# Sparse graph attention on one core: the units of each batch's first pair in another order, the average of v one place later, and a longer lead for the last projections

## The chip, the core and the metric

The kernel runs on one core of a Trainium2 chip. The metric is the device time of one launch in microseconds (us). A core has five engines that run side by side, each through its own list of instructions in a fixed order: PE (TensorE, matmuls), DVE (VectorE), ACT (ScalarE), POOL (GpSimd, which here issues the gathers) and SP (SyncE, which issues plain transfers). An instruction that needs another engine's result waits for it, and all that stands behind it on its own engine waits too.

## The reference

One layer of attention over a graph, a residual and a normalisation, for 16 batches of 1024 nodes with 512 features and 8 heads of 64:

```python
q = (x @ Wq + bq).reshape(b, n, H, HD)
k = (x @ Wk + bk).reshape(b, n, H, HD)
v = (x @ Wv + bv).reshape(b, n, H, HD)
scores = jnp.einsum('bqhd,bkhd->bhqk', q, k) / jnp.sqrt(jnp.float32(HD))
scores = scores + (1.0 - adj)[None, None, :, :] * -1000000000.0
attn = jax.nn.softmax(scores, axis=-1)
out = jnp.einsum('bhqk,bkhd->bqhd', attn, v).reshape(b, n, d)
return out @ Wo + bo              # then layernorm(x + this)
```

adj is a 0/1 matrix of 1024 x 1024, the same for all batches, with few ones in most rows. All arithmetic that reaches the output is in fp32.

## The kernel before

**Data.** The kernel ranks the nodes by their number of edges and works on queries in that order, in 8 tiles of 128. A query has few keys, so instead of the whole score matrix the kernel gathers, for each tile, its first, second, third key and so on: one *block* is 128 queries with one key each. A block is one indirect transfer by POOL of 128 rows of k and v (`gather`, L1242), a product with q and a sum over each head on DVE (`products` L1263, `scores` L1267), an exponential on ACT (L1278), a weighting of v by ACT (eight small activations, L1291) or by DVE (L1295), and an addition on DVE (L1307) or, for the few queries with many keys, a matmul on PE (L1316, L1317). There are 530 blocks in all, 32 or 34 for each batch; a query without any edge takes the mean of v, which the kernel keeps as one more row of the table of k and v.

**Projections ("fronts").** Before a batch's blocks can be gathered, its k, v and q must lie in DRAM. The function `pair(b, j)` computes them for two tiles of 128 rows (j = 0 to 3). k and v of two tiles come from seven products in place of eight (a scheme of sums and differences of half matrices): the units, in order, are x, p6, x again, p7, z, p4, z again. A unit is two matmuls of 128x128 by 128x512 in fp32, which stand as four rows in the profile. Between them stand q0 and q1 (the q products of the two tiles, four matmuls each) and xt (the two transposes of x that the next pair needs). x and z are each one PSUM bank that is filled in two halves: first a product, which must be read out (x by ACT's copy e, L960; z by DVE's L975, which makes v of the second tile), and then a second product added on top, read out again. So the second half of x waits for the copy e and the second half of z waits for L975. p6, p7, p4, all q and output products, the transposes, the average and others share four PSUM banks in turn (`fill_psum`).

In a batch's first pair (j = 0) from batch 1 on, q1 is empty. For even batches from 2 on q0 is empty too; for odd batches from 3 on q0 is the q product of a tile that two batches share, followed by `lone_product`, four bf16 matmuls.

After a batch's last pair `add_v` adds the last v tiles to vsum (L854), and `mean_pe` multiplies it by 1/N (matmul pm, L858); ACT copies the row and SP stores it (L864), and only then is the batch marked as set up, so that its blocks can be gathered.

**Outputs.** A finished tile is normalised (L1337), transposed (poT, L1351), multiplied by Wo (po, L790), added to x and normalised by DVE, ACT and POOL, and scattered to its rows. Twenty tiles are spilled to DRAM and finished after the fronts have ended.

**Order.** The whole order is written by one loop over *places* n, one for each block: at each place the loop emits the block work of nearby blocks, then what was put off to this place (`later(k, ...)` means k places on), and then PE work of fronts or outputs (`finish`) until a credit of PE time, `share`, is used up. `urgent` holds short PE work that goes ahead of it. A front unit has a condition (the second halves need e or v1 to have been emitted); if it is not met the place ends there. The share is set at each batch's first block, so that the fronts reach a given lead: `ahead` = 13 (EARLY) plus up to 11 (FIRST) places, less from batch to batch, beyond the batch after next. From batch 13's blocks on the share is what is left of the fronts, spread up to `fronts_end`, 12 places ahead of the last batch's first block. Gathers run 8 places ahead (AHEAD), 11 after the fronts' end (AHEAD_LAST), and not before the batch is set up. For odd batches from 3 on the first gather is `more` (L1217), which reads the table of both batches of a pair.

Of the kernel before, what the change touches and what calls it, by code (L numbers as in the profile page):

```python
# [46 lines left out]
LATE = 12  # L47
# [130 lines left out]
def kernel(  # L178
# [37 lines left out]
    B, N, D = x.shape  # L216
# [37 lines left out]
    with ExitStack() as main:  # L254
# [185 lines left out]
        now, plan, rest, urgent, known, waiting, combined = [0], {}, {}, [], [], [], []  # L440

        def later(k, fn):
            plan.setdefault(now[0] + k, []).append(fn)
# [363 lines left out]
        def pair(b, j):  # L807
# [25 lines left out]
            def send(i):  # L833
                assert b < PAIRED_FROM or gathered[0] >= start[max(0, b // 2 * 2 - 2)]
                kv = KV[b, tt[i]]
                rows, base = kv_of(b)
                for lo, hi in ((0, LONE), (LONE + P, 2 * P)) if b and tt[i] == 0 else ((tt[i] * P - (LONE if b and tt[i] == 1 else 0), None),):
                    hi = lo + P if hi is None else hi
                    part = slice(0 if lo % P == 0 or hi - lo == P else LONE, P if hi - lo == P or lo else LONE)
                    later(1, lambda lo=lo, hi=hi, part=part: nc.sync.dma_start(rows[base + lo:base + hi, :], kv[part, :]))  # L840
                R["sent"] = R.get("sent", 0) + 1
                if R["sent"] == 2:
                    later(1, add_v)
                    if j == NT // 2 - 1:
                        later(2, lambda: urgent.append(mean_pe))

            def add_v():
                kv = [KV.pop((b, t))[:, D:] for t in tt]
# [56 lines left out]
            if j == 0 and b >= PAIRED_FROM:  # L905
                q0 = []
# [29 lines left out]
            def a(i, h):  # L936
                return XT[b, tt[i]][:, ts(h, HD2)]

            def unit(bank, left, right, first, after, need):
                def pe():  # L940
                    if first:
                        R[bank] = fill_psum(f"p{bank}_{b}_{j}") if bank[0] == "p" else psum.tile(
                            [P, HALF], F32, tag=bank, name=f"{bank}_{b}_{j}", bufs=1
                        )
                    l = left()
                    for c in range(2):
                        nc.tensor.matmul(  # L947
                            R[bank], l[:, ts(c, P)], right[:, c, :], start=(first and c == 0), stop=(c == 1),
                            skip_group_check=True,
                        )  # L950
                    later(1, after)

                return [(2 * PRODUCT, pe, lambda: (need is None or need in R) and (b, j) in SX and bool(combined))]
# [28 lines left out]
            def s(i):  # L982
                return lambda: SX[b, j][i - 1]

            units = []
            units += unit("x", lambda: a(0, 0), B11, True, out_e, None)
            units += unit("p6", s(2), T2, True, out_w, None)
            units += q0
            units += unit("x", lambda: a(0, 1), B21, False, lambda: out_k(0, R["x"]), "e")
            units += unit("p7", s(3), T3, True, out_g, None)  # L990
# [472 lines left out]
        with tc.manual_schedule():  # L1463
# [9 lines left out]
            def needed(b, part):  # L1473
                b += int(part)
                if b >= B:
                    return fronts_time
                return fronts_by[b - 1] + (part - int(part)) * (fronts_by[b] - fronts_by[b - 1])

            finishing, last_finish, reloads, last_reload = [], -LEAD_IN, 0, 0
            fronts_end = start[B - 1] - 12  # L1480
            credit = 0.0
            for t in range(3):
                load_x(0, t)
# [1 line left out]
            while n < total or plan or rest or urgent or done or finishing or spilled or lone_tiles or not guarded:  # L1485
                now[0] = n
                if n < 0:
                    share = START_SHARE if n > FRONT_BY else LEAD_SHARE if n > -LEAD_IN else TRANSPOSE * 1.5
                elif n >= start[LATE + 1]:

                    share = sum(u[0] for u in fronts) / max(fronts_end - n, 1) + NS * SUM / NBT if fronts else LAST_SHARE
                elif n in start:

                    b = start.index(n)
                    left = sum(u[0] for u in fronts)
                    ahead = EARLY + FIRST * (1 - max(0, b - 1) / LATE)
                    goal = fronts_time - needed(b + 2, ahead / NBT)
                    kept = sum(number(b, t) not in SPILL for t in tiles_of(b))
                    share = (max(0.0, left - goal) + kept * NPAIR * PRODUCT + NS * SUM) / (start[b + 1] - start[b])
                if 0 <= n + 3 < total:  # L1500
                    exponentials(n + 3)
                if 0 <= n + 4 < total:
                    products(n + 4)
                while gathered[0] < min(n + (AHEAD if fronts else AHEAD_LAST) + 1, total) and blocks[gathered[0]][0] in set_up:
                    gather(gathered[0])
                    gathered[0] += 1
                if 0 <= n + 1 < total and not by_act(n + 1):
                    weigh(n + 1)
                if 0 <= n < total and blocks[n][2] < OWN[blocks[n][1]]:
                    add_own(n)  # L1510
                if 0 <= n + 4 < total:
                    scores(n + 4)
                if 1 <= n <= total and (n == total or blocks[n][2] == 0):
                    normalise(*blocks[n - 1][:2])
                if 0 <= n < total and blocks[n][1:] == one_key_at(blocks[n][0]):
                    turn(blocks[n][0], ONE_KEY, V1.pop(blocks[n][0]))
                if 0 <= n < total and blocks[n] == (B - 1, *MORE_AT):
                    turn(B - 1, MORE_TILE, V1.pop("more"))
                for fn in plan.pop(n, ()):
                    fn()  # L1520
                if 0 <= n + 2 < total and by_act(n + 2):
                    weigh(n + 2)
                for fn in rest.pop(n, ()):
                    fn()
                credit += paced(share, n) if n >= 0 else share
                if 0 <= n < total and blocks[n][2] >= OWN[blocks[n][1]]:
                    add_up(n)
                    credit -= SUM
                for tile_done in done[:0 if fronts and len(done) < LAZY else 1 if fronts else 2] + coming:
                    if tile_done not in loaded and kept_y() < 5:  # L1530
                        load_y(*tile_done)
                if lone_tiles and kept_y() < 4:
                    load_lone(lone_tiles.pop(0))
                coming[:] = [t for t in coming if t not in loaded]
                if spilled and not fronts and n > last_reload + 1 and len(Y) - kept_y() < 7:
                    reload(*spilled.pop(0), reloads)
                    reloads, last_reload = reloads + 1, n
                first_unit = True
                while credit > 0 or urgent:
                    if urgent and not (first_unit and fronts):  # L1540
                        urgent.pop(0)()
                        continue
                    if (
                        not finishing and len(done) > (LAZY if fronts else 0) and n > loaded.get(done[0], n) + 1
                        and n > last_finish + bool(fronts) and not total - 2 <= n < total
                    ):
                        finishing = finish(*done.pop(0))
                        last_finish = n
                    units = finishing or fronts
                    if not units:  # L1550
                        if urgent:
                            urgent.pop(0)()
                            continue
                        break
                    cost, fn, ready = units[0]
                    if ready and not ready():
                        if urgent:
                            urgent.pop(0)()
                            continue
                        break  # L1560
                    del units[0]
                    fn()
                    credit -= cost
                    first_unit = False
                credit = min(credit, 2 * share)
                while known and waiting:
                    load_x(*waiting.pop(0))
                preps += prep.pop(n, [])
                preps = [g for g in preps if next(g, True) is None]
                n += 1  # L1570
# [34 lines left out]
```

## Time and profile before

| | |
|---|---|
| median of 3 runs | 1875.09 us (1874.72 to 1876.87) |
| the profiled execution | 1894.52 us, of which the span from the first to the last instruction is 1892.4 |
| VectorE busy | 1695.3 us |
| ScalarE busy | 1557.4 us |
| POOL busy | 1262.6 us |
| q and output products (pq, po) on PE | 748.6 us |
| seven-product units (x, pp, z) on PE | 834.8 us in the page's groups |
| mean granted TensorE clock | 0.990 |

The profiled execution is some 19 us longer than the runs that give the time; sums are made against it. In lists of waits the columns are total us, times, longest. In a timeline each line is start and duration in us, engine, line of the kernel, operation, what it writes and reads, shapes, a count, and in brackets the idle time of the engine just before it and who ended it. In tables of stretches each engine has its busy us and instruction count; the last columns are the granted TensorE clock, the share of the DMA engines and GB/s. TensorE's ends are modelled, so small differences between busy shares carry little.

The page by slices shows the three stages: a setup until some 150 us, a long middle in which PE, DVE and ACT are all near full, and from some 1725 us a tail without fronts.

```profile
PE   7979999999999999999999999999999999999996
...
DVE  6888879999998999899999989899999989997875
ACT  3627868988888988988898878988899989977885
POOL 1366765777676776767676766767676866656884
PEclk9989999999999999999999999999999999999998
```

### The profile page before, as it was taken

What the parts mean: (1) busy time and instruction counts of PE and PEld (TensorE: products, weight loads), DVE (VectorE), ACT (ScalarE), POOL (GpSimd) and SP (SyncE); (2) the same over time, 40 slices, a digit from 0 to 9 for tenths busy, and PEclk for the clock granted to TensorE, in tenths of its full rate; (3) what the DMA queues carried; (4) which work ended last, traced back from release to release, by engine and by line L of the source; (5) the groups of instructions that cost most, each with busy time, mean ns of one, the idle gap of its engine ahead of it and who ended that gap; (6) DMA issues with size and microseconds to landing.
All of it is one profiled execution on the core that took longest, in us unless ns stands there. A gap on an engine that the chain in (4) does not pass through costs nothing. (4 is left out here: it accounts for less than half of the span.)

```text
span 1892.4 us, 25171 instructions
## 1 busy us (share of the span) xinstructions
PE 1816.5 (96%) x5149; PEld 876.6 (46%) x5149; DVE 1695.3 (90%) x3470; ACT 1557.4 (82%) x6128; POOL 1262.6 (67%) x1189
## 2 busy tenths in 40 slices
PE   7979999999999999999999999999999999999996
PEld 3434444444545454444444444444545444444442
DVE  6888879999998999899999989899999989997875
ACT  3627868988888988988898878988899989977885
POOL 1366765777676776767676766767676866656884
PEclk9989999999999999999999999999999999999998
DMA  7356786888989897989889897989889899989993
GB/s 279 115 167 215 226 290 229 309 298 291 322 266 319 303 333 256 345 290 310 299 284 329 279 324 261 334 303 309 286 302 352 297 332 319 329 282 319 340 332 137
DMA packets 188149, 544.63 MB, mean 288 GB/s; under 512 B 32602, under 2 KB 32622, under 8 KB 187986
## 3 DMA queue, kind: packets, MB, share of 16 engines
q0 software_dynamic: 116400, 382.82, 60.4%
q1 hardware_dynamic: 68510, 154.30, 21.7%
q10 hardware_dynamic: 3076, 5.82, 0.8%
q14 instruction: 120, 0.98, 0.2%
q8 instruction: 43, 0.70, 0.2%
HBM read 419.52 MB, written 144.34 MB: 298 GB/s over the span
## 5 line engine op out<-in xcount | busy, mean ns | idle before, releaser
L1291 ACT ACTIVATE pv<-kvg,pv 128x64 f32<-128x64 f32 x3544 | 893.4, 340 | 1.8 <-issue 1.8
L1242 POOL DMA_INDIRECT kvg<-kv_pair,place_row x462 | 522.6, 1131 | 258.6 <-issue 94.5
L790 PE MATMUL po<-wo,oT 128*128 128x512 f32 x816 | 379.2, 600 | 2.0 <-DVE vsum L854 1.2
L790 PE MATMUL pq<-wq,xT 128*128 128x512 f32 x792 | 369.4, 598 | 1.3 <-DVE s L1267 0.8
L1267 DVE TENSOR_REDUCE s<-qk 128x8 f32<-128x512 f32 x530 | 360.8, 681 | 7.2
L1263 DVE TENSOR_TENSOR qk<-qt,kvg 128x512 f32<-128x512 f32 x434 | 296.8, 684 | 13.2 <-DMA kvg<-kv_pair,place_row 13.1
L947 PE MATMUL x<-b,xT 128*128 128x512 f32 x504 | 239.0, 597 | 0.1
L947 PE MATMUL pp<-t,s 128*128 128x512 f32 x504 | 237.3, 593 | 1.5 <-DVE t L383 1.5
L1307 DVE TENSOR_TENSOR pv<-pv,pv 128x520 f32<-128x520 f32 x329 | 228.4, 694 | 8.2 <-ACT pv L1291 8.0
L790 PEld LDWEIGHTS po<-wo,oT 128*128 128x128 f32 x816 | 153.4, 192 | 171.7 <-issue 162.7
L790 PEld LDWEIGHTS pq<-wq,xT 128*128 128x128 f32 x792 | 149.0, 192 | 169.3 <-issue 157.7
L1001 POOL DMA_INDIRECT x<-in_x_dram,asked_row x120 | 129.6, 1080 | 103.5 <-PE pxT L748 35.4
L1278 ACT ACTIVATE pv<-s,absent 128x8 f32<-128x8 f32 x434 | 126.8, 293 | 55.1 <-DVE s L1267 36.6
L1125 POOL DMA_INDIRECT out_dram<-y,asked_row x129 | 145.1, 1125 | 35.9 <-issue 25.0
L800 ACT ACTIVATE sq_k<-kv 128x128 bf16<-128x128 f32 x512 | 150.8, 300 | 8.4 <-DVE kv L970 4.5
L947 PEld LDWEIGHTS x<-b,xT 128*128 128x128 f32 x504 | 95.3, 192 | 111.6 <-issue 105.2
L947 PEld LDWEIGHTS pp<-t,s 128*128 128x128 f32 x504 | 94.1, 190 | 111.3 <-issue 102.2
L947 PE MATMUL z<-b,s 128*128 128x512 f32 x252 | 121.4, 604 | 13.1 <-DVE kv L975 10.4
L1196 POOL DMA_INDIRECT qg<-q_rows,query_row x96 | 105.5, 1099 | 28.5 <-issue 25.3
L1029 POOL DMA_INDIRECT y<-in_x_dram,asked_row x93 | 105.0, 1129 | 26.1 <-issue 25.8
L947 PE MATMUL z<-t,s 128*128 128x512 f32 x252 | 118.6, 593 | 0.0
L947 PE MATMUL pp<-t,xT 128*128 128x512 f32 x252 | 118.5, 592 | 0.0
(276 smaller groups left out, 2750.2 us busy)
## 6 DMA issues: line engine op xcount, KB each, us to landing
kv_pair<-kv SPq DMA_DIRECT2D x98, 512.0 KB
q_rows<-q SPq DMA_DIRECT2D x106, 256.0 KB
qt<-q_rows SPq DMA_DIRECT2D x98, 256.0 KB
residual<-x SPq DMA_DIRECT2D x36, 256.0 KB
y<-residual SPq DMA_DIRECT2D x36, 256.0 KB
kv_rows<-kv SPq DMA_DIRECT2D x15, 512.0 KB
kvg<-kv_pair,place_row POOLq DMA_INDIRECT x462
kv_pair<-kv SPq DMA_DIRECT2D x28, 256.0 KB
```

Source lines behind the costliest of these rows:

```text
L790: nc.tensor.matmul(p, lhs(c), w[:, c, :], start=(c == 0), stop=(c == NPAIR - 1))
L800: nc.scalar.activation(sq, s[:, ts(h, P)], AF.Square, scale=scale, accum_out=sums[:, h:h + 1])
L947: nc.tensor.matmul(R[bank], l[:, ts(c, P)], right[:, c, :], start=(first and c == 0), stop=(c == 1), skip_group_check=True,)
L1001: nc.gpsimd.indirect_dma_start(out=y, out_offset=None, in_=x_rows, in_offset=bass.IndirectOffsetOnAxis(ap=asked_row[:, t:t + 1], axis=0), ...
L1125: nc.gpsimd.indirect_dma_start(out=out_rows[b, t], out_offset=bass.IndirectOffsetOnAxis(ap=rows, axis=0), in_=y, in_offset=None, element_o ...
L1196: nc.gpsimd.indirect_dma_start(out=q, out_offset=None, in_=q_rows[b % ROWS], in_offset=bass.IndirectOffsetOnAxis(ap=rows, axis=0))
L1242: nc.gpsimd.indirect_dma_start(out=KG[n], out_offset=None, in_=rows, in_offset=bass.IndirectOffsetOnAxis(ap=(place_row if b else key_row)[ ...
L1263: nc.vector.tensor_tensor(QK[n], q, KG[n][:, 0:D], op=OP.mult)
L1267: nc.vector.tensor_reduce(S[n], QK.pop(n).rearrange("p (h d) -> p h d", d=HD), axis=AX.X, op=OP.add)
L1278: nc.scalar.activation(PV[n][:, D:], S.pop(n), AF.Exp, bias=bias)
L1291: nc.scalar.activation(pv[:, ts(h, HD)], v[:, ds(D + h * HD, HD)], AF.Copy, scale=pv[:, D + h:D + h + 1])
L1307: nc.vector.tensor_tensor(PV[b, t], PV[b, t], pv, op=OP.add)
```

## The change

Three edits. In the first pair of each batch from 2 on, q0 is replaced by the first of the two x transposes, the place of xt is left empty, and the former q0 (with `lone_product`, where there is any) and the second transpose go between z's first half and p4. `mean_pe` is put off by three places instead of two for every batch but the first. And the fronts end 16 instead of 12 places ahead of the last batch, while `ahead` grows by 2 places at batch 11's first block and by 4 at batch 12's.

```diff
                 if R["sent"] == 2:
                     later(1, add_v)
                     if j == NT // 2 - 1:
-                        later(2, lambda: urgent.append(mean_pe))
+                        later(3 if b else 2, lambda: urgent.append(mean_pe))
...
             units = []
             units += unit("x", lambda: a(0, 0), B11, True, out_e, None)
             units += unit("p6", s(2), T2, True, out_w, None)
+            if j == 0 and b > 1:
+                q0, q1, xt = xt[:1], q0 + xt[1:], []
             units += q0
             units += unit("x", lambda: a(0, 1), B21, False, lambda: out_k(0, R["x"]), "e")
             units += unit("p7", s(3), T3, True, out_g, None)
             units += xt
             units += unit("z", s(1), T1, True, out_v1, None)
             units += q1
             units += unit("p4", lambda: a(1, 1), T4, True, out_k1, None)
             units += unit("z", s(4), B22, False, out_v0, "v1")
...
-            fronts_end = start[B - 1] - 12
+            fronts_end = start[B - 1] - 16
...
                     ahead = EARLY + FIRST * (1 - max(0, b - 1) / LATE)
+                    ahead += 2 * max(0, b - LATE + 2)
                     goal = fronts_time - needed(b + 2, ahead / NBT)
```

In the changed kernel lines from 985 on stand two lines lower, and the last ones three.

## The prediction

> **What bounds the kernel now.** I read the page's busy times first, then the busy time by stretches, then the waits of the tensor engine (PE), then the timelines at the batch boundaries. Page, then stretches:
>
> ```profile
> PE 1816.5 (96%) x5149; PEld 876.6 (46%) x5149; DVE 1695.3 (90%) x3470; ACT 1557.4 (82%) x6128; POOL 1262.6 (67%) x1189
> ...
> 300.00:1700.00 1400.00, 1372.04 (x3931) 666.46 (x3930) 1316.60 (x2578) 1240.91 (x5019) 971.05 (x897) 1.00 0.88 305
> ...
> 1535.00:1570.00 35.00, 30.11 (x85) 13.99 (x84) 31.04 (x59) 27.19 (x108) 22.73 (x22) 0.95 0.93 326
> ```
>
> From 300 to 1700 us PE is busy 98%, VectorE (DVE) 94%. PE's work is fixed, so time is won only by removing PE's idle stretches: 28 us of those 1400. DVE is nearly full too, so a stretch removed here can come back at the next thing DVE owes. The third line is the worst stretch: PE idles 4.9 of 35 us and part of it runs at half clock. Who ends PE's waits (us, times, longest):
>
> ```profile
> PE z L947 <- DVE kv L975: 10.4, 5, 3.9
> ...
> PE pm L858 <- DVE vsum L854: 2.7, 3, 1.2
> ...
> PE pxT L748 <- DVE q L821: 1.6, 2, 0.8
> ...
> PE po L790 <- DVE vsum L854: 1.2, 1, 1.2
> ...
> PE pm L858 <- ACT oT L1355: 1.1, 1, 1.1
> ```
>
> The largest is the second half of z, which adds to a bank that DVE must first read (L975). PE at batch 10's first pair:
>
> ```profile
> 1090.39 1.88 PE L947 MATMUL z<-t,s 128*128 128x512 f32 x4
> 1092.10 1.88 PE L947 MATMUL pp<-t,xT 128*128 128x512 f32 x4
> 1097.85 2.61 PE L947 MATMUL z<-b,s 128*128 128x512 f32 x4 [3.86 <-DVE kv L975]
> 1100.24 3.00 PE L947 MATMUL x<-b,xT 128*128 128x512 f32 x4
> ```
>
> Only one unit of 1.72 us stands between the halves. After the wait x takes 3.00 instead of 1.88: the clock was halved. And at batch 13's boundary POOL stops:
>
> ```profile
> 1520.93 0.87 POOL L1113 TENSOR_TENSOR stats<-stats,neg_half 128x1 f32<-128x1 f32 x1
> 1526.75 1.96 POOL L1217 DMA_INDIRECT more<-kv_pair,place_row  x1 [4.95 <-issue]
> ```
>
> SP issued the mean row's store at 1522.68; the gather from the same table starts 4.1 us later.
>
> **What the Trainium skill says.** "TensorE: Matmul & The Clock Gate", Part 1 (the HAM clock gate): the array falls to half rate after an idle window of about 3.4 us, and the window runs free. The trace shows the half rate (3.00 for 1.88), but it also follows idle stretches shorter than a window, 2.67 us before 877; so I price it from the trace: a half-clock stretch of 3.4 us loses 1.7. Same page, Architectural detail: VectorE and ScalarE are strict FIFO. Agrees: L975 stands behind a whole place's DVE work. "DMA: Bandwidth & Descriptors", Two DMAs through the same engine are not ordered: a dependent DMA has to wait for the first one's completion. That is the 4.95 us above.
>
> **The change part by part** (times of the profiled execution).
>
> *1. First pairs, batches 2 to 15.* No instruction is added. In even batches one x transpose (4 matmuls, 0.44 us) moves from ahead of the first half of z to between z's halves, the other to between p6 and the second half of x. In odd batches q0 (3.44) and lone_product (0.9) also move between z's halves. In the timelines of before, seven first pairs waited at z's second half: batches 4, 6, 7, 8, 10, 11, 12 with 0.54, 1.23, 1.34, 2.67, 3.86, 0.83, 1.45, in sum 11.9 us. In the changed program's order the PE work between the halves, at 0.86 per unit matmul, is 6.4 to 14.6 us in the odd batches (1.7 to 6.0 before), and 7.3 in batch 10, where sums and an output product fall in between: 7, 10 and 11 lose their 6.0. In 4, 6, 8 and 12 it grows only from 1.71 to 2.15: 4 x 0.43 = 1.7 gained, 4.2 left. Batch 14 shrinks from 3.4 to 2.15, and L975 now stands behind a whole place of DVE work; batch 12, with the same four operations ahead, had L975 end 3.3 after z's half, plus two y operations 1.3 = 4.6, so a new wait of 2.4 (0 to 3). Net -5.3 (range -9 to -2).
> Two half-clock stretches follow these waits, at 877 and 1099. The second goes, -1.7; the first stays, as batch 8 keeps 2.2 us.
> New tight places. (a) In odd batches q0 and lone_product no longer lie between x's halves, where ScalarE's copy e must come first. PE reaches the second half 4.3 us after x's start in batches 3, 7, 11, 13, 7.3 or later in 5, 9, 15. Before, e ended 4.5, 2.5, 3.6, 5.2 us after x's start in those four: waits 0.2 and 0.9, +1.1. (b) Four PSUM banks rotate; in batch 3 the transpose takes q0's bank 0.86 us after q0's last matmul, in batch 7 p4 takes it after 1.72. DVE's q (L821) must have read it a place later; the trace's two such waits (pxT <- q) are 0.8 each, with more PE work between. L975 lagged 1 to 6 us in first pairs; I take 2.0 and 1.0: +3.0 (0 to 8). x rows for the earlier transpose were gathered 40 us ahead in every batch, SP's order is nearly unchanged and DVE's four sums of halves (L774 to L777) now follow z: all nothing.
>
> *2. mean_pe a place later (b > 0).* vsum was late at 310, 1086, 1298, 1622 and 1731: 2.7 + 1.2 + 1.1 from the waits = -5.0 (-5 to -3). Its row is stored a place later; first gathers run 8 places ahead, and up to batch 12 the row still comes 12 or more places ahead, so four are left.
>
> *3. More lead for the last batches.* Counting places, the mean row of batches 13, 14, 15 comes 12, 12, 11 ahead of the batch's first block instead of 9, 8, 8. So the POOL stop of 4.95 (2.86 at batch 15) goes. Behind it stood two x gathers and the next key gathers; DVE then waited for keys at 1538.7 and 1543.3 (1.47, 1.53), and PE idled 0.66 at 1541.9, 1.63 at 1558.8, 2.46 at 1565.4, with 1.7 lost to half clock: 6.5 us. DVE's own backlog made part of these; I take two thirds, -4.3 (-6.5 to 0). Fronts end four places earlier; outputs move into the tail, where PE is the bound as well, so nothing; one output product takes the bias matmul, +0.2.
>
> Sum: -5.3 - 1.7 - 5.0 - 4.3 = -16.3; +1.1 + 3.0 + 0.2 = +4.3; net -12.0. DVE has 6% of its time free against PE's 2%, and in stretches (1570 to 1610: 39.3 of 40 us) nothing; there a gain comes back as a wait for DVE. I take 0.6 of the net: -7.2 us. The profiled execution took 1894.5 (span 1892.4), 19.4 above the median of the runs, 1875.1; I carry the difference over unchanged: 1867.9, say 1868.
>
> **The rivals.**
> - *DVE takes it back.* For: 94% busy, and most of PE's other waits end on DVE (poT <- o, sum <- pv). Against: DVE itself idles 83 us of the 1400, much of it waiting for PE. With 0.15 of the net, -1.8: 1873.
> - *Slower: x's second half waits for e.* Place: batches 3, 7, 11, 13, where the cover of 7 to 12 us is gone. If ScalarE is as late as the 7.1 us seen once (batch 5, third pair), each costs 2.8 plus a halved clock, 4.5: 18 us against 7.2: 1886. It decides from 1.8 us per place, e ending 6.1 after x's start. Against: among these four e ended at most 5.2 after.
> - *All of it.* The waits left in part 1 vanish as DVE is less behind, part 3 gives its 6.5 and nothing new appears: 11.9 + 3.4 + 5.0 + 4.8 (less the half clock counted) = 25; three quarters of that, -19: 1856.
> - *It does not do what it says:* in five even batches the halves stay only 2.15 apart; that is in the sum already.
>
> **How the numbers follow.** Main case 0.52 (1863 to 1872), taken back 0.22, e late 0.15, all of it 0.11. What the measurement can tell from no change is 0.2%, 3.75 us. Faster: the main case nearly whole (0.48), all of it (0.11), a little of the second (0.01): 0.60. Slower: e late, 0.15. Same: 0.25. For 8 in 10 the range reaches to "taken back" and a light form of "e late", and down to near "all of it": 1856 to 1878.
>
> **What would show it.** PE's waits for kv L975 fall from 10.4 to some 4 to 7, what is left lies in batches 4 to 14, even; pm's waits for vsum are gone; POOL's stop before L1217 (line 1219 after) is under 1 us; PE's busy share in 1535 to 1570 rises. Against it: ACT e named as what ends PE's waits for x, longer pxT <- q waits, more half-clock stretches between 200 and 1750 us than the four of before (at 266, 877, 1099, 1566), or the same idle sum under new names. I am wrong if PE's idle time between 200 and 1750 us does not fall by at least 5 us.

## The result: slower by 0.3%, and the profile after

The changed kernel takes 1881.92 us (median of 11 runs, 1877.68 to 1890.9) against 1875.57 of the kernel before beside it (11 runs): ratio 1.003, with an interval from 1.0019 to 1.0042. The prediction was 1868, with a range up to 1878; the time lies above both. A loss of 0.3% is small, but it is there, and it came back both times that the change was repeated: 1.0031 (1.0013 to 1.005) in e16 and 1.0042 (1.0028 to 1.0056) in e17.

The kernel before took 1875.6 to 1877.3 us in four of the six sessions of runs, 1897 and 1909 in the two others, and 1894.5 in the profile used for the prediction, so every ratio is to runs of the same session and traces are compared here with a repeat of the kernel before (e1, span 1875.6) and not with that profile.

This is the busy time of the changed kernel in two stretches (the stretch, its length, the busy time of PE, of its weight loads, of DVE, ACT and POOL, then granted clock, DMA share and GB/s):

```profile
300.00:1700.00 1400.00, 1380.48 (x3955) 672.26 (x3961) 1322.61 (x2583) 1241.64 (x5034) 976.46 (x899) 1.00 0.88 307
1535.00:1570.00 35.00, 35.00 (x103) 17.19 (x102) 34.55 (x68) 32.24 (x133) 21.44 (x21) 1.00 0.92 328
```

The same view of the repeat of the kernel before:

```profile
300.00:1700.00 1400.00, 1378.29 (x3956) 671.28 (x3955) 1323.32 (x2586) 1244.65 (x5041) 973.89 (x902) 1.00 0.88 307
1535.00:1570.00 35.00, 31.42 (x88) 14.62 (x87) 34.41 (x67) 29.35 (x116) 19.78 (x20) 0.95 0.88 300
```

Against the profile used for the prediction PE gains 8.4 us of busy time between 300 and 1700 us; against the repeat it gains 2.2. The stretch of batch 13 is as forecast (35.00 of 35 us), and already in the repeat it was less bad than the 30.11 I started from. These lines say who ends PE's waits in the changed kernel (us in total, times, longest):

```profile
PE pp L947 <- DVE s L776: 7.9, 4, 4.6
PE z L947 <- DVE kv L975: 6.6, 5, 2.6
...
PE poT L1353 <- DVE ends L1347: 5.8, 1, 5.8
PE sum L1318 <- DVE pv L1297: 4.7, 3, 2.2
PE po L790 <- DMA oTs<-spill: 3.0, 1, 3.0
...
PE pm L858 <- DVE vsum L854: 1.4, 1, 1.4
```

And in the repeat of the kernel before:

```profile
PE z L947 <- DVE kv L975: 8.5, 7, 3.9
...
PE pm L858 <- DVE vsum L854: 2.7, 3, 1.1
...
PE pm L858 <- ACT oT L1355: 1.1, 1, 1.1
```

Of the lines that are new, three are large: PE waits for a sum of halves (s, L776) 7.9 us, for the last attention block (poT, released by DVE's L1347) 5.8 us, and for the reload of a spilled tile 3.0 us. The first comes from edit 1, the others from edit 3, as the experiments below show. The longest wait of the first kind lies again in batch 10's first pair. Here is PE, and then DVE, of the changed kernel:

```profile
1078.22 0.60 PE L748 MATMUL pxT<-ident,x 128*128 128x128 f32 x4
1078.66 1.88 PE L947 MATMUL pp<-t,xT 128*128 128x512 f32 x4
1080.38 1.88 PE L947 MATMUL z<-b,s 128*128 128x512 f32 x4
1082.10 1.88 PE L947 MATMUL x<-b,xT 128*128 128x512 f32 x4
1083.81 0.60 PE L1353 MATMUL poT<-ident,o 128*128 128x128 f32 x4
1088.98 3.75 PE L947 MATMUL pp<-t,s 128*128 128x512 f32 x4 [4.57 <-DVE s L776]
```

```profile
1084.71 0.69 DVE L970 TENSOR_TENSOR kv<-pp,g 128x512 f32<-128x512 f32 x1
1085.31 0.68 DVE L1265 TENSOR_TENSOR qk<-qt,kvg 128x512 f32<-128x512 f32 x1
1085.91 0.69 DVE L1297 TENSOR_TENSOR pv<-kvg,pv 128x512 f32<-128x512 f32 x1
1086.51 0.72 DVE L1309 TENSOR_TENSOR pv<-pv,pv 128x520 f32<-128x520 f32 x1
1087.16 0.67 DVE L1269 TENSOR_REDUCE s<-qk 128x8 f32<-128x512 f32 x1
1087.76 0.41 DVE L774 TENSOR_TENSOR s<-xT 128x256 f32<-128x256 f32 x1
1088.09 0.41 DVE L775 TENSOR_TENSOR s<-xT,xT 128x256 f32<-128x256 f32 x1
1088.42 0.41 DVE L776 TENSOR_TENSOR s<-s,xT 128x256 f32<-128x256 f32 x1
```

z's second half (1080.38) no longer waits, as forecast. But the second transpose now runs at 1078.22. Its sums of halves (L774 to L777) stand on DVE behind a place of other work, which runs without an idle gap, and they start only at 1087.76. The second pair's p6 needs the third of them, L776, so PE stands idle for 4.57 us and then runs at half clock (3.75 us for a unit of 1.88). In the repeat of the kernel before, both transposes ran at 1068.84, and DVE did the same sums beside z's first half, well before z's second half at 1084.24:

```profile
1078.77 0.44 DVE L774 TENSOR_TENSOR s<-xT 128x256 f32<-128x256 f32 x1 [2.88 <-PE z L947]
...
1079.47 0.41 DVE L776 TENSOR_TENSOR s<-s,xT 128x256 f32<-128x256 f32 x1
```

This is the end of the changed kernel on PE:

```profile
1755.67 1.98 PE L790 MATMUL po<-wo,oTs 128*128 128x512 f32 x4 [2.96 <-DMA oTs<-spill]
...
1850.94 0.70 PE L1318 MATMUL sum<-pv,sums 128*128 128x256 f32 x2 [1.48 <-DVE pv L1297]
1851.48 0.61 PE L1319 MATMUL sum<-pv,sums 128*128 128x264 f32 x2
1857.88 1.09 PE L1353 MATMUL poT<-ident,o 128*128 128x128 f32 x4 [5.80 <-DVE ends L1347]
...
1860.12 5.10 PE L790 MATMUL po<-wo,oT 128*128 128x512 f32 x8 [0.85 <-ACT oT L1357]
```

And this is the end of the repeat of the kernel before:

```profile
1849.87 1.88 PE L790 MATMUL po<-wo,oTs 128*128 128x512 f32 x4
1851.58 0.59 PE L1316 MATMUL sum<-pv,sums 128*128 128x256 f32 x2
1852.02 0.61 PE L1317 MATMUL sum<-pv,sums 128*128 128x264 f32 x2
1854.88 0.66 PE L1351 MATMUL poT<-ident,o 128*128 128x128 f32 x4 [2.26 <-DVE o L1337]
...
1856.50 5.40 PE L790 MATMUL po<-wo,oT 128*128 128x512 f32 x8 [0.19 <-ACT oT L1355]
```

Before, products of reloaded tiles (oTs) lay between the last blocks' sums, up to 1851.58. After, they have run out at 1848.35, and PE waits for the last block's chain of work.

The wait at 1755.67 is for a reload that was issued late. In SyncE's list it stood behind the store of a mean output row (L1051), which waited 12.8 us for ACT's copy of that row; in the repeat the same store waited 6.6 us. SyncE in the changed kernel:

```profile
1736.58 0.43 SPq L1231 DMA_DIRECT2D qt<-q_rows  x1
1749.77 0.23 SPq L1051 DMA_DIRECT2D mean_rows<-out_mean  x1
...
1750.52 0.38 SPq L1057 DMA_DIRECT2D oTs<-spill  x1
```

The account can be kept with two points of the trace: the end of the last z, where the fronts end, and PE's last matmul. What lies between is the tail. Idle times in the table are PE's, all columns in us.

| profiled execution | last z ends | tail to PE's last matmul | PE's idle time from 200 us to last z | idle in the tail | span |
|---|---|---|---|---|---|
| before, repeated (e1) | 1707.8 | 154.1 | 21.7 | 8.8 | 1875.6 |
| changed kernel | 1701.1 | 164.1 | 21.1 | 15.8 | 1878.8 |
| edit 1 alone (e2) | 1711.6 | 154.9 | 26.4 | 9.8 | 1880.2 |
| edit 2 alone (e3) | 1708.0 | 154.5 | 20.6 | 9.0 | 1876.2 |
| edit 3 alone (e4) | 1702.1 | 166.5 | 20.2 | 14.0 | 1882.2 |
| edit 1, second transpose stays (e5) | 1702.5 | 154.2 | 19.0 | 9.3 | 1870.4 |

The changed kernel is 6.7 us earlier at the last z and takes 10.0 longer from there: +3.3, against a difference of the spans of 3.2.

Counting attention blocks by the start of their product with q on DVE shows where the time goes. After the last z 44 of the 530 blocks are still to come in the changed kernel, and 40 in the repeat, at 3.7 and 3.9 us of tail for each: the fronts end four blocks earlier, but only 6.7 us earlier. The last block starts 5.3 us later than in the repeat, and block 508 was already 6.1 us late. The 5.80 us that PE waits at the end are therefore not where the blocks fall behind; PE has then already done the products that it still had between the last blocks of the repeat.

### The profile page after: what moved, and what is told of

Read it like the earlier page. It is cut to its first block, busy times and chain, and to the rows that moved or that the text cites. A ratio compares the mean times of both kernels' runs of the same rounds, so it can differ in the third digit from the quotient of the medians.

```text
span 1878.8 us, 25132 instructions
## 1 busy us (share of the span) xinstructions
PE 1808.3 (96%) x5136; PEld 875.6 (47%) x5150; DVE 1696.1 (90%) x3469; ACT 1554.9 (83%) x6128; POOL 1263.1 (67%) x1189
## 3 DMA queue, kind: packets, MB, share of 16 engines
q1 hardware_dynamic: 68510, 154.30, 21.7%
## 5 line engine op out<-in xcount | busy, mean ns | idle before, releaser
L1198 POOL DMA_INDIRECT qg<-q_rows,query_row x96 | 101.5, 1058 | 28.3 <-issue 24.0
```

## The experiments

Times are medians, with the number of runs in brackets; ratios are to the kernel before in the same session. The parts alone come first, in one session (before: 1876.85).

**e1, the kernel before once more** (no edit).

> The kernel before, unchanged, for a second trace. If the profile that the prediction was read from was an unusually long execution (1894.5 us against a median of 1875.6), this trace spans 1872 to 1878 us, the TensorE waits at z's second half sum to clearly less than the 11.9 us counted there, and the 4.95 us stop of POOL at batch 13 is shorter or gone. If profiling itself lengthens this kernel, it spans about 1892 us again with the same waits.

Measured: 1877.68 us in one run, span 1875.6. The profile of before was no fair picture of the kernel: PE's idle time from 200 us to the last z is 21.7 us here and 30.2 there, and z's waits from batch 4 on sum to 8.1 us here and 11.9 there. Only POOL's stop at batch 13 is nearly what it was: 4.47 us, after 4.95. There was a sign in the first profile. Among ScalarE's waits it has this line:

```profile
ACT e L960 <- issue: 32.5, 11, 8.5
```

These are eleven waits for which the profile names no releaser. The repeat has none of them for e; its longest wait there, also 8.5 us, ends on PE's x:

```profile
ACT e L960 <- PE x L947: 72.7, 32, 8.5
```

I summed ScalarE's idle gaps above 0.6 us whose releaser the profile cannot name. The profiled executions of the sessions around 1876 have 1.8 to 2.9 us of them; those of the sessions at 1897 and 1909, and the profile of before, have 36 to 57 us. The label is no cost by itself, but it tells such executions apart.

**e2, edit 1 alone.**

```diff
+            if j == 0 and b > 1:
+                q0, q1, xt = xt[:1], q0 + xt[1:], []
```

> First edit alone (the units of the first pairs). Prediction's step: faster by 3 to 5 us (ratio 0.998). Rival, pair theory: the second transpose now comes after z's first half, so the sums of halves for the second pair are late and its p6 waits for them (7.9 us in four waits in the changed kernel's trace, with one half-clock stretch): slower by 2 to 6 us (1.001 to 1.003). Tail theory: this edit is not the cause, 0.997 to 1.000.

Measured: 1881.19 us (13), ratio 1.0022 (1.0014 to 1.003): the edit that carried most of my gain loses by itself. This is PE in batch 10:

```profile
1084.91 0.60 PE L1353 MATMUL poT<-ident,o 128*128 128x128 f32 x4
1090.03 2.87 PE L947 MATMUL pp<-t,s 128*128 128x512 f32 x4 [4.52 <-DVE s L776]
```

Waits for s L776 sum to 9.1 us (five, 1.6 or less but for this one). z's waits fall to 3.4, from 8.1. A second kind of wait is new as well, for DVE's reading of q (L821), whose PSUM bank the next product takes over:

```profile
PE pp L947 <- DVE q L821: 3.5, 2, 2.4
```

It stops p4 in the first pairs of batches 13 and 15, for 1.09 and 2.41 us; with a third, of 0.42 us, the waits for q sum to 3.9 us.

**e3, edit 2 alone.**

```diff
-                        later(2, lambda: urgent.append(mean_pe))
+                        later(3 if b else 2, lambda: urgent.append(mean_pe))
```

> Second edit alone (mean_pe one place later). Prediction's step: faster by 2 to 4 us (0.998 to 0.999). Rival: the mean row of the last three batches comes only 8, 7 and 7 places ahead of the first block, so gathers of these batches start later and DVE waits for keys: slower by 2 to 5 us (1.001 to 1.003).

Measured: 1877.23 us (14), ratio 0.9995 (0.9985 to 1.0004): no difference, and neither of the two expectations. The four waits it takes away (0.45, 1.06, 1.07 and 1.15 us in e1, 3.7 in sum) are gone, but instructions next in line wait instead: po for y 1.55 us at 305.5, where the repeat has 0.45 and 0.80, and z for kv 2.62 us at 1298.1, where it has 1.06 and 1.45.

**e4, edit 3 alone.**

```diff
-            fronts_end = start[B - 1] - 12
+            fronts_end = start[B - 1] - 16
...
+                    ahead += 2 * max(0, b - LATE + 2)
```

> Third edit alone (fronts end four places earlier, more lead from batch 11). Prediction's step: faster by 2 to 4 us (0.998 to 0.999). Tail theory: TensorE runs out of output products before the last blocks, so it idles 6 to 8 us more after 1750 us and ends at half clock: slower by 4 to 8 us (1.002 to 1.004). Pair theory: no slower than before.

Measured: 1884.0 us (6), ratio 1.0045 (1.0031 to 1.0058): the dearest of the three parts. POOL's stop before the gather of L1217 is gone:

```profile
1516.00 0.87 POOL L1217 DMA_INDIRECT more<-kv_pair,place_row  x1 [0.31 <-issue]
```

But the tail of PE ends as in the changed kernel:

```profile
1860.64 1.08 PE L1351 MATMUL poT<-ident,o 128*128 128x128 f32 x4 [5.79 <-DVE ends L1345]
...
1862.87 5.74 PE L790 MATMUL po<-wo,oT 128*128 128x512 f32 x8 [0.85 <-ACT oT L1355]
```

By the table the last z is 5.7 us earlier and the tail 12.4 longer. Of these, 5.2 are idle time and 7.2 busy. The busy time before the last z falls by 3.7, so about 3.7 of the 7.2 is work that moved into the tail. Most of the other 3.5 goes with the half clock. In the tail PE is busy 12.4 us at half clock (in the halved stretches at 1757.8, 1836.3 and 1856.8 of the trace's clock records), where e1 has 6.8 (at 1832.8 and 1856.7). By estimate, counting half of that time as lost, this costs 6.2 us against 3.4. Block 504 starts 5.0 us later than in e1, block 506, after a wait of 3.07 us for a reload, 8.1 us, and the last block again 8.1 us.

The second session took the losses apart (before: 1877.29).

**e5, edit 1 with the second transpose left in its place.**

```diff
+            if j == 0 and b > 1:
+                q0, q1, xt = xt[:1], q0, xt[1:]
```

> First edit with one part undone: the second x transpose of a first pair stays ahead of z's first half; only the first transpose and q0 move. If the late sums of halves are what the first edit costs (waits of p6 for DVE L776, 9.1 us in five waits in its trace, with one half-clock stretch), these waits are under 1 us in all and the kernel takes 0.998 to 1.000 of before. Rival, the shared PSUM banks or the copy e: the waits for DVE q (3.9 us) and e stay and the ratio stays at 1.001 to 1.003.

Measured: 1871.78 us (6), ratio 0.997 (0.9957 to 0.9982), faster than the kernel before. No wait for s L776 is left. These are batch 10's first and second pair:

```profile
1073.49 1.88 PE L947 MATMUL pp<-t,xT 128*128 128x512 f32 x4
1079.31 3.20 PE L947 MATMUL z<-b,s 128*128 128x512 f32 x4 [3.94 <-DVE kv L975]
1082.30 2.40 PE L947 MATMUL x<-b,xT 128*128 128x512 f32 x4
1084.55 1.88 PE L947 MATMUL pp<-t,s 128*128 128x512 f32 x4
```

So the place of the second transpose is worth 0.5% between e2 and e5. That is not yet the price of the late sums alone: the 3.9 us of waits for q in e2 are gone in e5 too, so this pair of runs does not separate the sums from the shared banks. And z still waits 3.94 us in batch 10: with only q0 behind z's first half the even batches keep their wait (the waits at z are 7.3 us in sum from batch 4 on, against 8.1 in e1). In the odd batches z's wait is gone (1.08 and 0.52 us in batches 7 and 11). These waits don't explain the gain over e1: PE's idle time up to the last z falls by 2.7 us and the span by 5.2, and where the rest comes from is open.

**e6, only the earlier end of the fronts.**

```diff
-            fronts_end = start[B - 1] - 12
+            fronts_end = start[B - 1] - 16
```

> Of the third edit only the earlier end of the fronts (16 instead of 12 places ahead), not the lead from batch 11 on. Tail theory: the fronts end at the same place, outputs run out just as early, ratio 1.003 to 1.005 and again some 14 us of TensorE idle time after the last z. Rival, the cost lies in the denser batches 11 and 12: ratio 0.999 to 1.001.

Measured: 1885.93 us (5), ratio 1.0043 (1.0029 to 1.0056): the whole price of edit 3. The tail is 168.4 us long, with 17.5 us of idle time where e1 has 8.8. The wait for the last block is 5.79 us again, and the wait for the late reload is 4.82 us, longer than in e4. Block 504 starts 5.0 us later than in e1, block 506, after that reload, 10.2 us, and the last block again 10.2 us. The greater lead of batches 11 and 12 shows no gain or loss beside it.

**e7, edit 3 with the reloads spread** (every fourth reload of a spilled tile a place later, so that products last longer).

```diff
-                if spilled and not fronts and n > last_reload + 1 and len(Y) - kept_y() < 7:
+                if spilled and not fronts and n > last_reload + 1 + (reloads % 4 == 3) and len(Y) - kept_y() < 7:
```

> The whole third edit, with the reloads of spilled tiles spread so that one more place lies between two of them after every fourth: output products then last until the last block. Tail theory: the wait of 5.8 us before the last transpose and the 2.2 and 1.1 before sums shrink to some 5 in all, with less half clock at the end: ratio 1.001 to 1.002 instead of 1.0045. Rival, the tail is slow for another reason (contention of transfers): stays at 1.004 or more.

Measured: 1881.07 us (15), ratio 1.0023 (1.0015 to 1.0031): half the loss. The last block's wait shrinks,

```profile
1861.48 1.12 PE L1351 MATMUL poT<-ident,o 128*128 128x128 f32 x4 [3.80 <-DVE o L1337]
```

the waits for reloads shrink too (2.0 us in two), and one at 1758.0 grows (3.36 us, 1.13 at the like place of e1). So when the reloads are issued matters, but the run does not tell the products that run out from the reload that comes late. Its profiled execution, 1885.0 us, is longer than its median and gives no finer sum.

**e8, edits 1 and 2.**

> First and second edit together, without the third. If the parts add: 1.0022 - 0.0005, about 1.0017 (1.001 to 1.0025). If the second edit helps only where the first has made room (the average's product falls between z's halves): 0.999 to 1.001; the whole change would then be this plus the third edit's tail.

Measured: 1882.48 us (18), ratio 1.0027 (1.0019 to 1.0035), above both expectations: edit 2 does not help edit 1.

The third session fell on a chip where the kernel before took 1897.2 us (59 runs), and its intervals are 0.3 to 0.5% wide.

**e9** is the change with the second transpose left in its place (the line of e5 for that of edit 1), **e10** is e5 and edit 2, **e11** moves only the former q0, and **e12** is e5 with fronts that end later. The lines of e11 and e12:

```diff
+                q0, q1, xt = [], q0, xt
...
-            fronts_end = start[B - 1] - 12
+            fronts_end = start[B - 1] - 10
```

> The whole change with its one late piece undone: the second transpose stays ahead of z's first half, second and third edits as they are. If the late sums are what turned the change from a gain into a loss, this takes 0.998 of before (0.9965 to 0.9995), that is 1.003 less the 0.005 between the first edit with and without the late transpose. Rival, the tail of the third edit outweighs all: 1.001 or more. If the second and third edits keep their stand-alone costs (-0.0005 and +0.0045) on top of 0.997: 1.001.

> First edit with the second transpose staying, plus the second edit, without the third. If waits for the average only move to the next thing that DVE owes: the same as without the second edit, 0.997 (0.996 to 0.998). If the average a place later gains its 5 us here: 0.9945 to 0.9955.

> Only q0 and the bf16 products move between z's halves; both transposes stay where they were before. If the gain of the first edit comes from the odd batches' z waits alone: about 0.997 to 0.998, as with the first transpose moved too. If spreading the transposes matters: 0.999 to 1.000.

> First edit with the second transpose staying, and the fronts' end moved the other way, 10 instead of 12 places ahead of the last batch. Tail theory: outputs last longer in the tail, TensorE idles less there, but the last batch's mean row comes later and DVE waits for its first keys: within 0.002 of 0.997; gain only if the tail is short of outputs as it is. Prediction's step on lead: slower than 0.997 by 0.001 or more.

Measured, in this order: 1.003 (1.0013 to 1.0047), 0.9995 (0.9972 to 1.0018), 1.0001 (0.9982 to 1.002) and 1.0015 (0.9997 to 1.0032). The gain of e5 does not show in any of them: all four lie above its 0.997, so the comparisons that e10, e11 and e12 were made for can't be read from these four runs. And e9 is as slow as the whole change, as if the second transpose were worth nothing in it. So it was run again beside the change itself, in two more sessions (before: 1909.0 and 1877.0).

> Edit 1 with the second transpose left where it was, repeated. Theory A (the late sums of halves were what edit 1 cost, and its gain at z is real): ratio 0.997 again, 0.995 to 0.999. Theory B (the first gain belonged to that chip): 0.999 to 1.001.

> All three edits, the second transpose left where it was. Theory A (parts add: gain at z -0.3%, tail +0.45%): ratio 1.001 to 1.002, below the whole change's. Theory B (the tail decides alone): as the whole change, 1.003. Theory C (the tail's cost and the second transpose's cost are one and the same lateness): 0.998 to 1.000.

> As the run before, but the fronts end at 12 places as in the kernel before. Theory A (the earlier end of the fronts carries the whole cost of edit 3): 0.4% below the run before, ratio 0.997 to 0.998. Theory B (the greater lead in batches 11 and 12 costs as well): within 0.2% of the run before.

> The changed kernel unaltered, beside the three others on one chip. Theory A: ratio 1.003 again. Theory B (its loss belonged to that chip): 0.999 to 1.001.

> The changed kernel once more, beside the next run. Theory A: ratio 1.003 to the kernel before. Theory B: nearer to 1.

> All three edits, the second transpose left where it was, beside the changed kernel itself. Theory A (the late second transpose is the larger half of the loss in the whole change too): 0.4 to 0.7% below the run before, ratio 0.996 to 0.999. Theory B (the tail decides, the transpose is worth nothing within the whole change): within 0.2% of the run before, ratio 1.002 to 1.004.

| run | session's before | ratio | interval |
|---|---|---|---|
| e13, as e5 | 1909.0 | 0.9996 | 0.998 to 1.0013 |
| e14, as e9 | 1909.0 | 0.9958 | 0.9943 to 0.9973 |
| e15, e9 with `fronts_end` at 12 | 1909.0 | 0.9963 | 0.9944 to 0.9982 |
| e16, the change | 1909.0 | 1.0031 | 1.0013 to 1.005 |
| e17, the change | 1877.0 | 1.0042 | 1.0028 to 1.0056 |
| e18, as e9 | 1877.0 | 1.0016 | 1.0007 to 1.0025 |

Side by side in one session, the change with its second transpose left in place is 0.26% faster than the change (e18 against e17), between the two expectations for e18, and 0.7% faster in the session at 1909 (e14 against e16), where e14 lies below all that was expected of it. In e18 the waits for s L776 are gone (8.0 us in e17) and waits for q are as good as absent in both (0.3 us), so here it is mainly the late sums that differ; part of the gain is lost again at z, whose waits are 11.0 us against 6.8. In the sessions around 1877 the parts then add: -0.30 (e5), -0.05 (e3) and +0.45 (e4) make +0.10%, and e18 measured +0.16 (0.07 to 0.25). But the -0.30 was measured once, in six runs. In the two long sessions the parts don't add: e9 and e14, the same program, differ by 0.7%, e5's gain did not come back in e13, and e15 equals e14, although the tail of its profiled execution is 156.6 us against 167.2, so the price of the earlier end of the fronts does not show there. What is different in these sessions stays open.

## Why the prediction was wrong

- *The base.* The sum was made against one profiled execution of 1894.5 us and its difference carried unchanged to a median of 1875. Some 8.5 us of the idle time that I set out to remove (30.2 against 21.7 up to the last z) are not in the repeat. My own test, that PE's idle time between 200 and 1750 us must fall by at least 5 us, shows it: it is 21.5 us after the change, 9.9 less than in that profile (31.4) and 1.4 less than in the repeat (22.9).
- *z's waits, -5.3.* Right in kind: edit 1 alone (e2) takes them from 8.1 to 3.4 us. After the whole change z waits 0.54, 0.71, 0.54, 2.62 and 2.24 us in batches 4, 6, 8, 12 and 14, in sum 6.6, which is what the steps gave (4.2 left and 2.4 new), but partly by luck. The new wait in batch 14 was laid to the first edit; e2 has none there, and edit 3 alone (e4) has one of 2.00. Batch 12 has 1.44 in e2 and 2.62 with edit 2 alone (e3). So the other two edits gave back most of what the first one took, and against the repeat z's waits fall by 1.5 us.
- *"DVE's four sums of halves (L774 to L777) now follow z: all nothing".* This is the step that failed in edit 1. They are not only later, they are the input of the second pair's p6, and behind z they queue after a place of DVE work: 7.9 us of waits in the changed kernel, 9.1 in e2, and the half clock after 1088. I had looked at what the second transpose needs, and not at who needs it. Its place is worth 0.26% in the whole change (e18 against e17) and 0.5% in edit 1 alone (e5 against e2, where waits for q go too).
- *x waiting for e, +1.1, and PSUM's banks, +3.0.* Nearly nothing in the changed kernel: x waits 0.09 us in batch 3, and has 0.46 and 0.70 us to spare in batches 10 and 11; no wait for q is left. With edit 1 alone both were there, and about as large as forecast: e2 has 0.82 us for e and 3.9 for q, the latter in other batches than I named. Why the other edits remove them was not tested. The rival "x's second half waits for e" had the right sign for the wrong reason: ScalarE's e decides nothing here.
- *mean_pe, -5.0.* With this edit alone the waits went, and came back at the next thing that DVE owed: e3 is 0.9995. In the whole change one wait for vsum, of 1.4 us, is left, where I had said none. I kept 0.6 of the net gain for such returns; for this edit it should have been near 0. "DVE takes it back" had this part right.
- *POOL's stop, -4.3.* The stop is gone, as forecast, and 1535 to 1570 is full. PE's gain there is 3.6 us against the repeat, whose stop is 4.47 us. But e2, without edit 3, has a stop of only 1.62 us and PE at 34.6 of 35 us, so much of this gain comes with edit 1 already, and how much of it hangs on the stop is not shown. Whatever it is, e4 as a whole loses.
- *"outputs move into the tail, where PE is the bound as well, so nothing".* This is the step that failed in edit 3, and the larger one: +0.43%, or 8.6 us, for the earlier end of the fronts by itself (e6). PE is the bound in the tail only as long as there are output products ready to do. In the changed kernel it idles 15.8 us there instead of 8.8: 3.0 for the late reload, and 5.8 before the last poT instead of 2.26, because the products have run out. In e4 and e6 the blocks are 5.0 us late by block 504, lose another 3.1 and 5.2 at the reload, and nothing at the end. Why they are 5.0 us late before that is open, and no run moved the reload's place in SyncE's list alone. The longer half clock at the end (10.2 us instead of 3.4) costs nearly nothing in the changed kernel: PE is busy in 4.3 us of it, and the last po takes 5.10 us against 5.40.
- *The sum.* e2, e3 and e4 add to +0.62%, the change measured +0.30 to +0.42. The halved stretches fall differently in each program (in the trace of the change two after 200 us up to the last block, in e4 five), and e2's waits for q are not in the change. These are two places where the parts can't add; that they are the whole of it is not shown.

## What to carry to other kernels

Before pricing an instruction that moves later, list its readers, and their readers, up to the engine that is the bound. Here the transpose moved by half a pair, and the sums that it feeds came a whole place of DVE work later. Work that fills waits at the end of a kernel runs out sooner when it starts sooner; look at the bound engine's idle time there before calling a move free, and at what stands ahead of a transfer in its queue. And run the kernel before a second time before counting its gaps: here more than a quarter of PE's idle time (8.5 of 30.2 us) was not in the repeat.

## What was not expected of the hardware

The same program on one core took 1875 to 1877 us in some sessions and 1897 and 1909 in others, with mean granted clocks of 0.987 to 0.991 and 0.984 to 0.993 in the profiled executions. The runs of the five sessions with experiments were on five chips, so a chip's part can't be told from a session's. In the traces the difference is not in one place but in many gaps: over all kernels, PE's idle time from 200 us to the last z is 18.9 to 26.9 us in the short sessions and 26.6 to 41.5 in the long ones.

The half clock came after short idle times also here. The Trainium skill ("TensorE: Matmul & The Clock Gate", Part 1) states an idle window of about 3.4 us; in the repeat of the kernel before, a halved stretch of 3.4 us begins at 1856.7, after gaps of only 2.26, 0.50 and 0.19 us on PE, and another at 1832.8, after a single gap of 1.88. Two gaps close together, of 0.92 and 2.02 us, the second ending at 916.4 in the same trace, were not followed by one. The halved stretches within these traces last 3.4, 6.8, 10.2 or 13.7 us, multiples of one length. After the wait of 4.57 us in the changed kernel the clock stays halved for 6.8 us, of which PE is busy 6.0: by estimate, counting half of that time as lost, it costs some 3.0 us more.
